# A Perceiver block on one core: self-attention keys and values of six batches as 26 block products, with sums on GpSimd and a new order in the last batch

## Chip, cores and metric
The kernel runs on one core of a Trainium2 chip, as one program. The metric is device time in microseconds (us), the median of the runs of a kernel. In the text TensorE is PE, VectorE is DVE, ScalarE is ACT, GpSimd is POOL and SyncE, which only issues transfers here, is SP; these are the names that the profile uses.

## The reference
Eight batches of 128 rows (width 512) pass three stages, all in float32 with a float8-rounded feed-forward:

```
x = x + xattn(layernorm(x), ctx)      # 8 heads of 64 over 2048 context rows of width 384
x = x + attn(layernorm(x))            # one head, 128 x 128 per batch, causal mask
x = x + ffn(layernorm(x))             # 512 -> 2048 -> 512, relu, e4m3 hidden values and w2

attn:  n = layernorm(x)
       logits = (n @ Wq + bq) @ (n @ Wk + bk).T ; mask above the diagonal
       probs = softmax(logits, axis=1) / sqrt(512)
       x = x + n + probs @ (n @ Wv + bv)
```

The change concerns the middle stage, `attn`: its keys and values.

## The kernel before
**Cross-attention** is a loop over batches b = 0 to 7 and head pairs m = 0 to 3. In each turn PE computes the scores of two heads (L552, 8 matmuls of 64x512), DVE copies them to `p` with running maxima (L556), ACT exponentiates each head in one instruction (L576), DVE transposes 32x32 blocks in place (L589, 8 instructions), and 16 transfers, the strips (L595, 128 KB each), put the blocks in their places in `pT`. `attend` (L607) of this pair comes one turn later on PE, after the scores of the next pair. Its first matmul waits for all 16 strips. `pT` has one buffer. Between `scores` and `attend` the keys and values of the next batch are computed by a block scheme of 20 products (L453, L476), from sums that POOL forms (`sum_half`, L206).

**Self-attention before** folds the query and key weights in one matrix (`both`), so "keys" is `both` times the normalised rows. Class `SelfAttention` works on two groups of four batches. Group 0 (batches 0 to 3): keys as 16 matmuls of 128x512 (L791) in turn m = 1 of the last batch, logits (L806) and three values (L835, 4 matmuls of 128x512 per batch) in turn m = 2. Group 1 (batches 4 to 7): values of 4 and 5 in and after turn m = 3, keys of 4 and 5 and of 6 and 7 as 16 matmuls of 128x256 each; batches 6 and 7 come last, since their rows are ready last. `read` (L858) multiplies probabilities by values. The normalised rows of batches 0 to 5 wait in DRAM (`xtd`, `xr`).

**The feed-forward** uses a block scheme of 26 products for 3/4 of the hidden blocks (`hidden_blocks`, L1162, tables `ROW_SUMS`, `WEIGHT_SUMS`, `PRODUCTS`): a 2x4 by 4x4 block product in 26 instead of 32 block products. It needs 19 sums of rows and 29 of weights (L1133), and its products run through six PSUM banks: a bank takes several products, and between two of them ACT (a block's first use, L1172) or DVE (later ones, L1175) reads it. The first quarter of the hidden units is plain (`hidden`, L1108).

**What sets the order.** PE's order is the order of the code (a manual schedule), and so is that of DVE and ACT. POOL and SP are ordered by a scheduler. Each engine and each queue takes its instructions in order, so an instruction that waits holds up all behind it. PSUM has seven banks for this work (`ps_one`) and one for the output of `attend`.

Around the change the code of the last batch reads, in `if last` branches: turn 0 `v_proj(7,1)` and `project(6)` (L717, output projection of batch 6), turn 1 `sa0.keys`, turn 2 `sa0.weights_and_values`, turn 3 the last loads; then the tail: values, `attend(7,3)`, `project(7)`, normalisation of batch 7 (`stats`, `scale`, `norm`), its keys and logits, the normalised rows of the feed-forward (`turned_rows`, L134), `hidden`, `hidden_blocks`. On DVE the weight and row sums of the feed-forward are placed among the self-attention steps by hand (`some(w_sums, n)`).

Of the kernel before, what the change touches and what calls it, by code (L numbers as in the profile page):

```python
# [65 lines left out]
def tile_perceiver_block(  # L66
# [39 lines left out]
    GT = GB * S  # L106
    RSK = float(D) ** -0.5
# [32 lines left out]
    ktp = ctx.enter_context(tc.tile_pool(name="ktp", bufs=1, side="right"))  # L140
    xa = ctx.enter_context(ExitStack())
# [5 lines left out]
    pp, ptp, tmp, xp = right("pp", 1), right("ptp", 1), right("tmp", TMPB), right("xp", 2)  # L147
# [389 lines left out]
    def scores(b, m):  # L537
# [8 lines left out]
        home, tag = (ktp, "kt0") if (b, m) == (B - 1, 2) else (pp, "p")  # L546
# [175 lines left out]
    rows = {}  # L722
    attention = ctx.enter_context(ExitStack())

    def bring_last_rows():
        rows[0] = keep.tile([P, B, D], F32, tag="keep", name="rows")
        nc.gpsimd.dma_start(rows[0][:, B - 2 :], xd[:, B - 2 :])
        for r in range(B):
            xs[r] = rows[0][:, r, :]

    def bring_rows():
        nc.scalar.dma_start(rows[0][:, : B - 2], xr[:, : B - 2])


    def load_row(pool, src, name):
        t = pool.tile([P, D], F32, tag=name, name=name)
        nc.gpsimd.dma_start(t, src if len(src.shape) > 1 else src.partition_broadcast(P))
        return t

    def load_columns(pool, src, name):  # L740
        t = pool.tile(list(src.shape), F32, tag=name, name=name)
        nc.gpsimd.dma_start(t, src)
        return t

    class SelfAttention:


        def __init__(self, g, lasting, pool, w):
            self.g, self.lasting, self.pool = g, lasting, pool
            self.both, self.swv, self.bv, self.u, self.mask = w  # L750
            self.rows = [g * GB + i for i in range(GB)]
            self.xt = lasting.tile([P, NK, GT], F32, tag=f"xt{g}", name=f"xt_{g}")
            there = slice(g * GT, min((g + 1) * GT, (B - 2) * S))
            nc.gpsimd.dma_start(self.xt[:, :, : there.stop - there.start], xtd[:, :, there])
            self.xn, self.es, self.vals = {}, {}, {}

# [12 lines left out]
        def norm(self, b):  # L769
            mv, sd = self.xn[b]  # L770
            rs = small.tile([P, 1], F32, tag="rs", name=f"rs_s_{b}", bufs=4)
            nc.vector.reciprocal(rs, sd)
            self.xn[b] = self.lasting.tile([P, D], F32, tag="xn", name=f"xn_s_{b}", bufs=GB + 1)
            nc.vector.tensor_scalar(self.xn[b], xs[b], mv[:, 0:1], rs, ALU.subtract, ALU.mult)
            nc.gpsimd.tensor_tensor(xs[b], xs[b], self.xn[b], ALU.add)
            unread = self.pool.tile([P, D], BF16, tag="unread", name=f"unread_{b}")
            row_constant(b, self.xn[b], self.u, unread)

        def turn(self, b):
            turned_into(self.xt, b, self.xn[b], "s")  # L780

        def keys(self, rows):

            at = slice(rows[0] % GB * S, (rows[-1] % GB + 1) * S)
            n = at.stop - at.start
            if at.start == 0:
                self.kt = self.pool.tile([P, NK, GT], F32, tag="sk", name=f"sk_{self.g}")
            for m in range(NK):
                ps = bank(f"psk_{rows[0]}_{m}")
                for k in range(NK):  # L790
                    nc.tensor.matmul(  # L791
                        ps[:, :n], self.both[:, k, ts(m, P)], self.xt[:, k, at],
                        start=(k == 0), stop=(k == NK - 1),
                    )
                nc.scalar.activation(
                    self.kt[:, m, at], ps[:, :n], AF.Identity, bias=side[:, m : m + 1]
                )
                if m == 1:
                    yield

        def logits(self, b):

            i = b % GB
            ps = bank(f"pl_{b}")
            for k in range(NK):
                nc.tensor.matmul(  # L806
                    ps[:, :S], self.kt[:, k, ts(i, S)], self.xt[:, k, ts(i, S)],
                    start=(k == 0), stop=(k == NK - 1),
                )
            lg = self.pool.tile([P, S], F32, tag="lg", name=f"lg_{b}", bufs=4)  # L810
            nc.vector.scalar_tensor_tensor(
                lg, ps[:, :S], c_rows[:, b : b + 1], self.mask, ALU.add, ALU.add
            )
            nm = small.tile([P, 1], F32, tag="snm", name=f"snm_{b}", bufs=4)
            nc.vector.reduce_max(nm, lg, axis=AX.X, negate=True)
            self.es[b] = lg, nm

        def exps(self, b):
            lg, nm = self.es[b]
            e = self.pool.tile([P, S], F32, tag="e", name=f"e_{b}", bufs=4)  # L820
            den = small.tile([P, 1], F32, tag="sden", name=f"sden_{b}", bufs=4)
            nc.scalar.activation(e, lg, AF.Exp, bias=nm, accum_out=den)
            self.es[b] = e, den

        def probabilities(self, b):
            e, den = self.es[b]
            r = small.tile([P, 1], F32, tag="sr", name=f"sr_{b}", bufs=4)
            nc.vector.reciprocal(r, den)
            nc.vector.tensor_scalar(e, e, r, RSK, ALU.mult, ALU.mult)
            self.es[b] = e  # L830

        def values(self, b):
            ps = bank(f"psv_{b}")
            for k in range(NK):
                nc.tensor.matmul(  # L835
                    ps, self.xt[:, k, ts(b % GB, S)], self.swv[:, k, :],
                    start=(k == 0), stop=(k == NK - 1),
                )

            v = self.pool.tile([P, D], F32, tag="sv", name=f"sv_{b}", bufs=GB + 2)  # L840
# [3 lines left out]
        def weights_and_values(self, rows):  # L844
            for r in self.rows:
                self.logits(r)
                self.exps(r)
            for r in rows:
                self.values(r)
            yield  # L850

        def reads(self):
            for r in self.rows:
                self.read(r)

        def read(self, b):
            ps = bank(f"pr_{b}")
            nc.tensor.matmul(ps, self.es[b], self.vals[b], start=True, stop=True)  # L858
            nc.vector.tensor_tensor(xs[b], ps, xs[b], ALU.add)
# [14 lines left out]

    def enter_self_attention():
        src.close()
        sap = ctx.enter_context(tc.tile_pool(name="sap", bufs=1, reuse_waits="tile"))
        wsa = attention.enter_context(tc.tile_pool(name="wsa", bufs=1, reuse_waits="tile"))
        both = wsa.tile([P, NK, D], F32, tag="both", name="both")
        nc.gpsimd.dma_start(both, both_w)  # L880
        w = [both, wsa.tile([P, NK, D], F32, tag="swv", name="swv")]
        sa0 = SelfAttention(0, sap, wsa, w + [None] * 3)
        nc.gpsimd.dma_start(w[1], sa_wv.rearrange("(k p) n -> p k n", p=P))
        w += [load_row(wsa, sa_bv, "bv"), load_row(wsa, u_line, "u")]

        mask = wsa.tile([P, P], F32, tag="mask", name="mask")
        nc.gpsimd.memset(mask, 0.0)
        nc.gpsimd.affine_select(
            out=mask, in_=mask, compare_op=ALU.is_ge, fill=MASKED, base=0,
            pattern=[[1, P]], channel_multiplier=-1,  # L890
        )
        w.append(mask)
        sa0.bv, sa0.u, sa0.mask = w[2:]
        return sap, wsa, w, sa0
# [58 lines left out]
    def normed_group(g, mv, sd, out):  # L953
        rs = small.tile([P, GB], F32, tag="qrs", name=f"frs_{g}")
        nc.vector.reciprocal(rs, sd)
        for i in range(GB):
            xn = sap.tile([P, D], F32, tag="xn", name=f"xn_f_{g}_{i}", bufs=GB + 1)
# [6 lines left out]
    def turned_rows(g, rows, tag):  # L964

        xt = sap.tile([P, NK, GT], F32, tag=tag, name=f"xf_{g}")
# [4 lines left out]
    sa0 = None  # L971
    for b in range(B):
        last = b + 1 == B
        for m in range(NK):
# [12 lines left out]
            if m == 3 and b < B - 2:  # L987
# [4 lines left out]
            elif b > 0:  # L992

                attend(b - 1, NK - 1)
            if m == 0:
# [5 lines left out]
            elif m == 1:  # L1001
                unit = sa0.keys(sa0.rows)
            elif m == 2:
                unit = sa0.weights_and_values(sa0.rows[:3])
            else:

                sa1 = SelfAttention(1, sap, wsa, w)
# [7 lines left out]
            else:  # L1015
                exps(b, m, 0)
                if unit and not (last and m > 0):
                    first_of(unit)
            if m == 3 and last:
                bring_rows()  # L1020
                for r in sa0.rows:
                    sa0.probabilities(r)
                sa1.stats(B - 2)
            exps(b, m, 1)
            if m == 3 and last:
                sa1.scale(B - 2)
            if b == m == 0:
                all_of(both_weights())
            if m == 0 and last:
                bring_last_rows()  # L1030
            if m == 1 and b > 0 and not last:
                row_stats(b - 1)
            if m == 2 and b > 0 and not last:
                norm_rows(b - 1)
            strips = turns(b, m)
# [7 lines left out]
            if m == NK - 1:  # L1043
                if last:
                    inverse_sums(b)
                else:
                    sums_along_rows(b)
            if unit:
                all_of(unit)
# [282 lines left out]
```

## Time and profile before

| | us |
|---|---|
| median of 3 runs | 1078.95 |
| lowest and highest run | 1078.9, 1079.66 |
| the profiled execution: device time | 1078.75 |
| its span, first to last instruction | 1077.0 |
| PE busy | 1069.6 |
| DVE busy | 782.9 |
| ACT busy | 373.4 |
| POOL busy | 262.1 |

All starts below are microseconds from the start of this span. In the tables of instructions each line gives an engine, a line of the kernel, an operation, out<-in with shapes and a count; then the busy time, the mean duration of one in ns, and the idle time just before, with what ended it. A float32 matmul appears as two matmul records, so x32 is 16 matmuls. The granted clock is 1.000 throughout.

### The profile page before, as it was taken

How to read it: one execution, taken by the hardware profiler on the slowest of the kernel's cores; microseconds unless marked ns; L12 is line 12 of the kernel's file. 1: busy time of each engine (PE TensorE's matmuls, PEld its weight loads, DVE VectorE, ACT ScalarE, POOL GpSimd, SP SyncE). 2: the span in 40 equal slices, each digit the busy share in tenths (PEclk: the TensorE clock that was granted, in tenths of full speed). 3: DMA queues.
4: the chain of work that ended last, by engine and by line, in shares of the span. 5: the costliest groups of instructions: out<-in, count | busy, mean ns of one | idle time of the engine just before them, and what ended most of it. 6: DMA issues, size and time to landing. Idle time of an engine off the chain costs nothing.

```text
span 1077.0 us, 15773 instructions
## 1 busy us (share of the span) xinstructions
PE 1069.6 (99%) x5586; PEld 701.0 (65%) x5586; DVE 782.9 (73%) x1724; ACT 373.4 (35%) x608; POOL 262.1 (24%) x397
## 2 busy tenths in 40 slices
PE   9999999999999999999999999999999999999998
PEld 5475784577467647754775578557746655758775
DVE  4876477778777778787778768777877758686654
ACT  3322233324332433432343234332433232256442
POOL 0254140361055005500550153026200221104000
PEclk9999999999999999999999999999999999999999
DMA  8466434553565456545643653455344745530001
GB/s 321 147 187 145 129 79 98 147 148 79 127 165 137 96 131 165 137 95 134 161 124 79 183 146 83 118 147 147 79 98 118 230 136 154 205 108 10 11 30 40
DMA packets 74031, 136.64 MB, mean 127 GB/s; under 512 B 29392, under 2 KB 37856, under 8 KB 72928
## 3 DMA queue, kind: packets, MB, share of 16 engines
q1 hardware_dynamic: 60736, 108.83, 39.5%
q10 hardware_dynamic: 9008, 15.73, 4.5%
q0 software_dynamic: 4208, 11.06, 3.5%
q8 instruction: 45, 0.74, 0.3%
q14 instruction: 34, 0.28, 0.1%
HBM read 55.85 MB, written 10.52 MB: 62 GB/s over the span
## 4 chain that ended last, share of the span: by engine, by line
PE 97%; DVE 1%; SPq 1%; ACT 1%; issue 0%; DMA 0%; POOL 0%; ACTq 0%; POOLq 0%
PE pv_z L476 22%; PE pk_z L453 20%; PE po L607 11%; PE sc L552 10%; PE ph L1162 7%; PE pv_b L476 4%; PE pk_b L453 3%; PE psk L791 3%; PE psv L835 3%; PE pq L520 3%; PE py L717 3%; PE pf L1190 2%; PE k L436 2%; PE ph L1108 1%; PE pw L336 1%; SPq L325 1%
## 5 line engine op out<-in xcount | busy, mean ns | idle before, releaser
L589 DVE STREAM_TRANSPOSE p<-p 128x512 f32<-128x512 f32 x256 | 158.9, 679 | 62.7 <-ACT p L576 62.7
L576 ACT ACTIVATE p<-p,nm 128x2048 f32<-128x2048 f32 x64 | 128.2, 2003 | 210.7 <-DVE nm L564 103.8
L556 DVE TENSOR_SCALAR_CACHE_REDUCE p<-sc 128x512 f32<-128x512 f32 x256 | 159.0, 686 | 20.7 <-PE sc L552 20.3
L476 PE MATMUL pv_z<-wv_sums,x_both 128*128 128x256 f32 x640 | 157.9, 381 | 0.0
L453 PE MATMUL pk_z<-x_both,wk_sums 128*128 128x512 f32 (+1 forms) x320 | 149.2, 572 | 0.9 <-ACT kt L369 0.6
L476 PEld LDWEIGHTS pv_z<-wv_sums,x_both 128*128 128x128 f32 x640 | 120.4, 190 | 18.6 <-issue 2.9
L607 PEld LDWEIGHTS po<-pT,v 128*64 128x64 f32 x2048 | 111.1, 137 | 23.8 <-issue 23.1
L607 PE MATMUL po<-pT,v 128*64 128x128 f32 x2048 | 118.9, 274 | 0.0
L552 PE MATMUL sc<-kt,q 64*128 64x512 f32 x512 | 118.5, 602 | 0.0
L476 PE MATMUL pv_z<-wv_sums,m_both 128*128 128x256 f32 x448 | 107.3, 379 | 0.0
L453 PEld LDWEIGHTS pk_z<-x_both,wk_sums 128*128 128x128 f32 x320 | 59.2, 190 | 67.1 <-issue 55.0
L453 PE MATMUL pk_z<-m_both,wk_sums 128*128 128x512 f32 (+1 forms) x224 | 101.3, 568 | 0.0
L629 POOL DMA_DIRECT2D line_s<-inverse x28 | 14.5, 526 | 352.4 <-DVE inverse L626 352.4
L206 POOL TENSOR_TENSOR m_both<-x_both 128x256 f32<-128x256 f32 x70 | 51.3, 733 | 172.7 <-DMA x_both<-in_ctx_t_dram 141.9
L476 PEld LDWEIGHTS pv_z<-wv_sums,m_both 128*128 128x128 f32 x448 | 84.2, 190 | 12.6 <-POOL x_both L206 0.8
L552 PEld LDWEIGHTS sc<-kt,q 64*128 64x128 f32 x512 | 46.8, 186 | 65.7 <-issue 54.3
L369 ACT COPY v<-pv_z 128x512 f32<-128x512 f32 x112 | 62.9, 586 | 56.1 <-PE pv_z L476 56.0
L369 ACT COPY kt<-pk_z 128x512 f32<-128x512 f32 (+1 forms) x112 | 59.8, 563 | 58.1 <-PE pk_z L453 57.7
L571 ACT COPY seen<-mx 128x1 f32<-128x1 f32 x21 | 4.0, 191 | 208.7 <-DVE p L556 208.7
L206 POOL TENSOR_TENSOR x_both<-x_both 128x256 f32<-128x256 f32 x98 | 70.7, 739 | 3.7 <-DMA x_both<-in_ctx_t_dram 3.6
L453 PEld LDWEIGHTS pk_z<-m_both,wk_sums 128*128 128x128 f32 x224 | 40.8, 190 | 46.8 <-issue 35.1
L372 DVE TENSOR_TENSOR v<-pv_z,v 128x512 f32<-128x512 f32 x96 | 63.1, 685 | 5.5 <-PE pv_z L476 5.5
(218 smaller groups left out, 1369.8 us busy)
## 6 DMA issues: line engine op xcount, KB each, us to landing
pT<-p SPq DMA_DIRECT2D x488, 128.0 KB, 2.4
x_both<-in_ctx_t_dram SPq DMA_DIRECT2D x45, 512.0 KB, 5.2
w<-in_w_t_dram ACTq DMA_DIRECT2D x2, 2048.0 KB, 11.3
w2f<-in_w_t_dram SPq DMA_DIRECT2D x16, 256.0 KB, 3.4
pT<-p POOLq DMA_DIRECT2D x24, 128.0 KB, 4.0
x_in<-in_x_dram SPq DMA_DIRECT2D x8, 256.0 KB, 6.5
qd<-xq SPq DMA_DIRECT2D x8, 256.0 KB, 3.0
q<-qd SPq DMA_DIRECT2D x8, 256.0 KB, 4.1
```

Source lines behind the costliest of these rows:

```text
L206: eng.tensor_tensor(x_block(b, h, to), x_block(b, h, one), x_block(b, h, two), ALU.add if op == "+" else ALU.subtract,)
L369: nc.scalar.copy(outs[ij], views(ps))
L372: nc.vector.tensor_tensor(outs[to], views(ps), outs[other], op)
L453: nc.tensor.matmul(ps[:, : n * BK], wk_sums[:, WSLOT[WAT[r]], f2, :], x_block(b, hs, XAT[r]), start=start, stop=True, skip_group_check=True,)
L476: nc.tensor.matmul(ps[:, ts(t, 256)], x[:, ts(t, P)], wv_sums[:, WSLOT[WAT[r]], :], start=start and t == 0, stop=True, skip_group_check=True,)
L520: nc.tensor.matmul(ps, wq[:, k, ts(m, P)], xt[:, k, :], start=(k == 0), stop=(k == NK - 1),)
L552: nc.tensor.matmul(pair[i], q[r, :], kts[b, m // 2][r, m % 2, ts(n, 512)], start=True, stop=True)
L556: nc.vector.tensor_scalar(p[:, :, i].rearrange("p g (t i) -> p t g i", i=SQ)[:, ts(n, Q)], pair[i].rearrange("p (t g i) -> p t g i", g=Q, ...
L576: nc.scalar.activation(p[:, :, i], p[:, :, i], AF.Exp, bias=nms[b, m][:, i : i + 1], scale=SCALE, accum_out=sums[b][:, h : h + 1],)
L589: nc.vector.transpose(p[:, g, i], p[:, g, i])
L607: nc.tensor.matmul(pos[b][h * DH : (h + 1) * DH, ts(m, P)].rearrange("p (a i) -> p a i", a=Q), v[:, jt % 8, ts(2 * m + h, DH)], turned_[b, ...
L1162: nc.tensor.matmul(banks[at][:, ts(t, HR)], w_at(of_w, d), x_at(g, of_x), start=start and t == 0, stop=True, skip_group_check=True,)
```

## The change
1. Keys and values of batches 0 to 5 (768 rows, two blocks of 384) are computed by the scheme of 26 products that the feed-forward has. Keys: 26 matmuls of 128x384 in turn m = 1 of the last batch. Values: 26 products of three matmuls of 128x128 each, in turn m = 3. The generator `product_blocks` is now shared with the feed-forward.
2. The sums that these products need (19 of rows, 29 of weights for the keys, 29 for the values) are made on POOL; one row sum that subtracts twice stays on DVE. The weights are summed in place, so plain `both` and `swv` are loaded a second time for batches 6 and 7, whose keys are now 16 matmuls of 128x128 each.
3. The self-attention tiles have no pools of their own: they are slices of `x_both`, `m_both`, `wk_sums` and `wv_sums`, which are free then. POOL and SP are ordered by hand from turn 0 of the last batch.
4. The last batch is rearranged: `project(6)` goes from the end of turn 0 to turn 1, ahead of the keys; batch 6 is normalised in turn 2 with its keys there; logits stand ahead of the strips' transposes in turns 2 and 3; reads 0 to 3 go behind `attend(7,3)`; `p` of turn 3 instead of turn 2 lies in a key tile.
5. In the tail fewer of the feed-forward's weight sums come ahead of `read`; the row sums start behind the last `read`.

The core of the diff, lines of the kernel after:

```diff
-        home, tag = (ktp, "kt0") if (b, m) == (B - 1, 2) else (pp, "p")
+        home, tag = (ktp, "kt0") if (b, m) == (B - 1, 3) else (pp, "p")
...
+    def product_blocks(name, mm, take, more, whole=None):
+        banks, taken, left = {}, set(), {}
+        for *_, reads in PRODUCTS:
+            for i, j, _ in reads:
+                left[i, j] = left.get((i, j), 0) + 1
+        for at, start, of_x, of_w, reads in PRODUCTS:
+            if start:
+                banks[at] = bank(f"{name}_{at}")
+            mm(banks[at], of_x, of_w, start)
+            for i, j, sign in reads:
+                (more if (i, j) in taken else take)(i, j, banks[at], sign)
+                taken.add((i, j))
+                left[i, j] -= 1
+                if whole and left[i, j] == 0:
+                    whole(i, j)
+            yield
...
+            for k in (2, 0, 1, 3):
+                nc.sync.dma_start(self.xt_six[:, k], xtd[:, k, :SIX])
+                nc.sync.dma_start(self.both[:, k], both_w[:, k])
...
+        def sum_w(self, w, some):
+            for to, one, op, two in some:
+                add_up(nc.gpsimd, self.w_at(w, to), self.w_at(w, one), op, self.w_at(w, two))
...
+        def keys_of_six(self):
+            def mm(ps, of_x, of_w, start):
+                nc.tensor.matmul(ps[:, :HALF], self.w_at(self.both, of_w), self.x_at(of_x),
+                    start=start, stop=True, skip_group_check=True)
+            def take(i, j, ps, sign):
+                nc.scalar.activation(self.kt_six[:, j, ts(i, HALF)], ps[:, :HALF], AF.Identity,
+                    bias=side[:, j : j + 1], scale=float(sign))
+            def more(i, j, ps, sign):
+                to = self.kt_six[:, j, ts(i, HALF)]
+                nc.vector.tensor_tensor(to, to, ps[:, :HALF], ALU.add if sign > 0 else ALU.subtract)
+            return product_blocks("psk", mm, take, more)
+        def values_of_six(self):
...
+                for t in range(3):
+                    nc.tensor.matmul(ps[:, ts(t, P)], x[:, ts(t, P)], self.w_at(self.swv, of_w),
+                        start=start and t == 0, stop=True, skip_group_check=True)
...
+            def whole(i, j):
+                for t in range(3):
+                    to = self.v_six[:, 3 * i + t, ts(j, P)]
+                    nc.gpsimd.tensor_tensor(to, to, self.bv[:, ts(j, P)], ALU.add)
...
+        def logits_and_keys(self):
+            self.turn(6)
+            self.logits(0)
+            yield
+            for b in range(1, 4):
+                self.logits(b)
+            self.keys(6, self.kts[6])
+            for b in range(4):
+                self.exps(b)
+            for b in range(4):
+                self.probabilities(b)
+        def logits_and_values(self):
+            for b in (4, 5):
+                self.logits(b)
+            yield
+            yield from self.values_of_six()
...
+            if m == 1 and last:
+                project(b - 1, ot)
...
-                unit = sa0.keys(sa0.rows)
+                unit = sa.keys_of_six()
             elif m == 2:
-                unit = sa0.weights_and_values(sa0.rows[:3])
+                unit = sa.logits_and_keys()
             else:
+                unit = sa.logits_and_values()
...
+            if m == 1 and b > 0:
+                (sa.stats if last else row_stats)(b - 1)
...
+            if m > 1 and last:
+                first_of(unit)
             strips = turns(b, m)
...
+            if m == 1 and last:
+                sa.scale(b - 1)
+                nc.scalar.activation(warm, eps, AF.Exp)
+                sa.load_plain(sa.both, both_w)
+                sa.sum_w(sa.swv, WEIGHT_SUMS)
...
-    some(w_sums, 16)
-    all_of(sa1.keys(sa1.rows[2:]))
...
+    sa.probabilities(B - 1)
+    xfs = [turned_rows(0, xf0, k_flat[:, : NK * GT])]
+    sa.read(B - 2)
     quantized = quantize_w2()
     hidden(0, xfs[0], range(1))
     some(quantized, 2)
-    for r in sa1.rows[2:]:
-        sa1.read(r)
...
+    sa.read(B - 1)
+    forms = wff.tile([P, 18, HR], F32, tag="x_forms_0", name="x_forms_0")
+    x_sums = form_x(0, xfs[0], [forms[:, i] for i in range(18)], nc.vector)
+    some(w_sums, 4)
     for _ in w_sums:
         some(x_sums, 1)
     all_of(x_sums)
```

## The prediction
> **What bounds the kernel now.** I read the table of busy time first, then the chain of waits, then the timeline and the stretches around the change.
>
> ```profile
> PE 1069.6 (99%) x5586; PEld 701.0 (65%) x5586; DVE 782.9 (73%) x1724; ACT 373.4 (35%) x608; POOL 262.1 (24%) x397
> ...
> PE 97%; DVE 1%; SPq 1%; ACT 1%; issue 0%; DMA 0%; POOL 0%; ACTq 0%; POOLq 0%
> ```
>
> PE is the bound, also in the chain. The chain's pieces (start, us, what) from 799 to 963.4 are PE alone, without a gap; some of them:
>
> ```profile
> 855.15 13.93 PE psk L791 x32
> 869.08 3.63 PE sc L552 x16
> 872.71 3.65 PE po L607 x64
> 876.36 3.77 PE pl L806 x32
> 880.13 10.30 PE psv L835 x24
> 890.43 3.63 PE sc L552 x16
> 894.06 3.64 PE po L607 x64
> 897.71 10.50 PE psv L835 x24
> ...
> 965.68 0.28 ACT sum L1172
> 965.96 0.04 issue
> 966.00 14.08 PE ph L1162 x64
> ```
>
> So a matmul saved here is worth its full time, and any new wait of PE here costs its full time: no slack is there to absorb it. The question is which is more.
>
> **What PE saves.** Keys and values take 13.93 + 10.30 + 10.50 in these pieces and 3.45 + 3.46 + 3.43 + 3.48 + 6.91 in five smaller ones behind them: 55.46 us. A matmul with 512 columns takes 13.93/16 = 0.870, with 256 columns 6.91/16 = 0.432, with 128 columns (`pl`) 0.89/4 = 0.224: proportional. After: 26 of 384 columns by 0.645 (three quarters of 0.86) = 16.8; 78 of 128 by 0.224 = 17.5; keys of batches 6 and 7, 32 by 0.224 = 7.2; their values 3.43 + 3.48 = 6.9. Sum 48.4, **7.1 less** (6.1 if a matmul of 128 columns costs 0.01 more than `pl` shows). PE's other matmuls stay the same in number; those moved cost what they did.
>
> **The new sums on POOL: nothing.** Not shown at these sizes. POOL's 128x256 sums take 0.735 and its 128x512 additions 1.274, which gives 0.46 for 128 columns and 1.0 for 384 by a line through them (0.23, as its `MEMSET` of 128x128, to 0.74 are the bounds of the first, 0.74 to 1.27 of the second). 16 row sums, 29 weight sums and two operations of the mask: about 31 us (20 to 44). Their loads (2.6 MB) go out on SP at about 820, when batch 7's key sums are used up, and by the 250 to 300 GB/s of the stretches below need 9 to 10 us. From 825 to 856, then. The keys begin at 855.1, since `project(6)` in front of them only changes place with them, take the sums in the order in which POOL makes them, and use the last at 871: 15 us of cover. The 29 sums of the value weights (13 us from 864) are used from 900 on, and the 24 bias additions (11 us) end by 922, before the first read at 923. Plain `both` comes back in 7 us after 871 and is used at 883.
>
> **The new waits on PE.** S is the start of scores(7,2), 873.2 with the sums so far and wait 1 below; R is the end of `rb`, about 923.2. DVE takes its instructions in the written order, and behind a turn's transposes come all the additions that free the banks.
>
> 1. Keys of six, **1.4** (0.9 to 1.9). On DVE the addition of `py` (waits for 855.1), statistics and the eight transposes of turn (7,1) (4.86, 856.7 to 861.6) stand ahead of the first addition, which ends at 862.1. The tenth product writes the same bank; PE would be there at 860.9.
> 2. `turn(6)`, **0.9** (0.5 to 1.2). It waits for `norm(6)` and its row constant, on DVE behind eight evictions of scores: ready at S + 8.0 and a hop; PE has done scores and attend at S + 7.3.
> 3. attend(7,2), **3.4** (2.0 to 4.5), the largest. The transfers that feed an attend now:
>
> ```profile
> 877.71 4.86 DVE L589 STREAM_TRANSPOSE p<-p 128x512 f32<-128x512 f32 x8 [2.16 <-ACT p L576]
> 882.86 2.89 POOL L595 DMA_DIRECT2D pT<-p  x6 [0.56 <-DVE lg L811]
> 893.99 3.71 PE L607 MATMUL po<-pT,v 128*64 128x128 f32 x64
> ```
>
> Columns: start, us, engine. And the stretches at that time, DMA share and GB/s last:
>
> ```profile
> 886.00:888.00 2.00, 2.00 (x6) 0.93 (x5) 0.69 (x1) 0.00 (x0) 0.00 (x0) 1.00 1.06 301
> 888.00:890.00 2.00, 2.00 (x6) 0.76 (x4) 0.00 (x0) 0.00 (x0) 0.00 (x0) 1.00 1.02 236
> 890.00:892.00 2.00, 2.00 (x9) 0.88 (x10) 1.17 (x2) 0.00 (x0) 0.00 (x0) 1.00 0.15 33
> ```
>
> The strips have landed near 890.1, 12.4 after the first transpose, 4 before they are needed. In that turn 25 us lie between the starts of scores and of this attend, filled by attend, logits and three values. After, scores, attend, `turn` 0.44, four logits 3.77, 3.58 of keys(6), the 0.9 above and scores(7,3) put PE there at S + 19.5. The first transpose stood 8.7 after the scores' start; now `norm(6)` and logits(0), which waits for PE's first `pl`, come first, so that it starts at S + 10.3. Add 12.4: S + 22.7, and a hop. PE waits 3.3 to 3.5. Should the strips land quicker in the quieter stretch it is 2; with POOL's strips held up by its weight sums, 4.5.
> 4. Values of six, **0.2** (0 to 1): logits 4 and 5 stand ahead of the transposes of turn (7,3), which end 5.5 us into the values; as in wait 1, but without `py`.
> 5. `ph_0`, **1.8** (0.5 to 2.5). PE's work between R and it: reads 0 to 3 3.43, `py` 3.43, reads 4 and 5 1.72, values 6.9, `turn` 0.44, logits 1.8, keys 3.58, `pt_f` 1.75, read(6) 0.86 = 23.9. ACT does exp(7) ahead of its copies of `pt_f`, and exp(7) waits for DVE's logits(7) behind ten weight sums of 0.55: R + 22.9. exp 0.4 and four copies (2.05 now) with their hops: R + 25.7.
> 6. First block of `hidden_blocks`, **3.4** (2.0 to 4.5). Now:
>
> ```profile
> 953.39 1.28 DVE L859 TENSOR_TENSOR rows<-pr,rows 128x512 f32<-128x512 f32 x2
> ...
> 960.87 0.42 DVE L1133 TENSOR_TENSOR x_forms<-x_forms,xf 128x256 f32<-128x256 f32 x1
> 961.21 1.28 DVE L942 BATCH_NORM_STATS2 fst<-rows 128x6 f32<-128x512 f32 x2
> ...
> 966.00 1.99 PE L1162 MATMUL ph<-x_forms,w_forms 128*128 128x256 f32 x8 [0.88 <-ACT sum L1172]
> ```
>
> Behind the last read DVE now has six weight sums, eleven row sums and statistics, ready 1 us before PE needs them. After, all 19 row sums and 19 weight sums stand behind read(7), a pair in 0.805 by the starts of these lines (0.47 + 0.34): 15.6, and 1.9 for the addition and statistics. read(7) ends one quarter of `hidden` after `ph_0`'s start; three quarters, 10.3, remain. The additions that the tenth product waits for (its bank again) come at 8.0 after the block's start; PE is there at 5.0 (968.70 now, from 963.43). That is 2.9, and 0.5 for the products behind.
>
> Sum: 1.4 + 0.9 + 3.4 + 0.2 + 1.8 + 3.4 = 11.1 of waits, less 7.1: **+4.0**. The profiled run took 1078.75 (span 1077.0 and 1.75 around it), so 1082.75; the median of before is 0.2 above that run, so about **1082.8**.
>
> [...]
>
> **The rivals.**
> - *Strips in time* (16%). Wait 3 falls, for the strips could land in 9 us rather than 12.4: 2.1 MB at the 301 GB/s of the stretch above are 7 us. Against it: the issuing itself, 16 strips over two queues, took until 886 now. 1082.8 - 3.4 = **1079.4**, no change.
> - *DVE's queue is not late at PE* (9%, faster). Waits 1, 2, 3, 4 and 6 (9.3) are all differences between an order on DVE and PE's arrival; if DVE runs 3 us further ahead than I place it, they go, and -7.1 + 1.8 = -5.3 remains: **1073.6**. It decides from waits of DVE under 5.3 in sum. For it: DVE is 73% busy. Against it: the transposes can't start before the exponentials, which hang on PE's scores, not on DVE's load.
> - *POOL late* (6%, slower). The loads come late or the sums take the upper bound, 44: the last ends at 870 rather than 856, each product waits in turn, and everything from the keys on shifts by up to 8: **1090** and more. It decides when the sums end past 868. Against it: the 15 us of cover.
> - That the change does not do what it says is excluded: 26 and 78 matmuls stand in PE's order.
>
> **How the numbers follow.** The forecast has the rest, 69%. Its lows are waits of 5.9 less 7.2, its highs waits of 15.6 less 6.1: from 1078.75 and with the 0.2, 1077.6 to 1088.5. That range also holds the even case, so that 15% is left out. 1076.8 to 1081.1 is within 0.2%, about what a measurement can tell from no change. Faster: 9%, the second rival. Same: 16%, the first. Slower: 69 + 6 = 75%.
>
> **What would show it.** In the profile after: `psk` and `psv` together at 48.4 on PE; PE idle 1.4 before the tenth key product, ended by DVE; 0.9 at `pt_s`, ended by DVE; 3.4 at attend(7,2), ended by a strip's DMA; 1.8 at `ph_0`, ended by ACT's copy of `xf`; 3.4 in the first `hidden_blocks`, ended by DVE; the last POOL row or weight sum of the keys near 856. Strips(7,2) landed by S + 19.5, or the last row sum within 2 us of the block's start, would make it wrong on the fast side; PE waiting for POOL at `psk` on the slow side.

## The result, and the profile after

The changed kernel takes **1089.22 us** (median of 4 runs, 1088.38 to 1091.89) against 1078.93 before: ratio 1.010, 95% interval 1.008 to 1.012, slower. The forecast was 1082.8 with a range of 1077.6 to 1088.5: the sign was right, the size was not. The profiled execution took 1088.51, span 1086.7, so 9.7 more than the 1077.0 before.

The page of the kernel after, busy time and chain:

```profile
PE 1067.4 (98%) x5714; PEld 710.8 (65%) x5714; DVE 798.2 (73%) x1755; ACT 380.0 (35%) x623; POOL 309.9 (29%) x488
...
PE 92%; DVE 5%; SPq 1%; DMA 1%; ACT 1%; issue 0%; POOL 0%; DVEq 0%; POOLq 0%
```

PE is busy only 2.2 us less, not 7.1, and the chain now runs 5% through DVE and 1% through a transfer. Who made PE wait from 840 to 1000, total, times, longest (before, this list held one line, 0.9 in the first product block):

```profile
PE po L611 <- DMA pT<-p: 5.8, 1, 5.8
PE ph L1264 <- DVE x_both L1277: 2.6, 1, 2.6
PE ph L1219 <- ACT wk_sums L137: 1.4, 1, 1.4
PE psk L863 <- DVE x_both L876: 1.2, 1, 1.2
PE ph L1264 <- DVE w L738: 0.9, 1, 0.9
PE pt_s L854 <- DVE pt_s L715: 0.8, 1, 0.8
PE psv L954 <- DVE mv_s L833: 0.2, 1, 0.2
```

All five places of the forecast with a wait of any size are there, with the releasers that it named. The first is the large one. Its transposes and its attend in the timeline (start, us, idle before in brackets):

```profile
883.93 4.86 DVE L593 STREAM_TRANSPOSE p<-p 128x512 f32<-128x512 f32 x8
...
899.68 6.12 PE L611 MATMUL po<-pT,v 128*64 128x128 f32 x64 [5.82 <-DMA pT<-p]
905.73 2.05 PE L931 MATMUL pl<-x_both 128*128 128x128 f32 x16
```

The same 64 records of attend take 3.71 in every other turn, 6.12 here. Stretches of 2 us (PE busy first; the last three columns are granted clock, share of the transfer engines, GB/s):

```profile
892.00:894.00 2.00, 1.86 (x6) 0.48 (x3) 2.00 (x8) 0.00 (x0) 0.46 (x1) 1.00 1.00 261
894.00:896.00 2.00, 0.00 (x0) 0.00 (x0) 2.00 (x7) 0.00 (x0) 0.00 (x0) 1.00 1.07 276
896.00:898.00 2.00, 0.00 (x0) 0.00 (x0) 1.29 (x6) 0.60 (x1) 0.00 (x0) 0.96 0.97 238
898.00:900.00 2.00, 0.32 (x4) 0.35 (x6) 0.00 (x0) 2.00 (x3) 0.00 (x0) 0.50 0.00 0
900.00:902.00 2.00, 2.00 (x22) 2.00 (x20) 0.00 (x0) 1.48 (x2) 0.00 (x0) 0.50 0.79 197
902.00:904.00 2.00, 2.00 (x23) 2.00 (x21) 0.00 (x0) 0.00 (x0) 0.00 (x0) 0.50 0.97 412
904.00:906.00 2.00, 2.00 (x29) 1.83 (x26) 0.00 (x0) 0.00 (x0) 0.00 (x0) 0.84 0.46 186
```

Two things are to be seen. The stretches show no traffic behind 898, but PE starts only at 899.68. The chain has what lies between (start, us, what):

```profile
892.93 5.98 DMA pT<-p
898.91 0.78 issue
899.68 6.12 PE po L611 x64
```

The last strip goes out at 892.93, its landing is noted at 898.91, and PE starts 0.77 behind it: the end of the traffic in the stretches is not yet the landing. And while PE stood idle here its granted clock fell to 0.50, and stayed there for 5 us after it had started again; PE is "busy" from 900 on, but at the pace of these 6.12. In the profile of before the clock is 1.00 throughout.

In numbers, profile against profile:

| step | forecast | measured |
|---|---|---|
| matmuls of keys and values (17.0 + 17.7 + 7.3 + 6.9 = 48.9) | -7.1 | -6.6 |
| 1, tenth key product | 1.4 | 1.2 |
| 2, `turn(6)` | 0.9 | 0.8 |
| 3, attend(7,2): wait | 3.4 | 5.8 |
| 3: half clock (attend 6.12 for 3.65) | none | 2.5 |
| 3: logits behind it, at full clock (1.98 for 1.79) | 0 | 0.2 |
| 3: scores(7,3) ahead of it (4.46 for 3.70) | 0 | 0.8 |
| 4, values of six | 0.2 | 0 |
| 5, `ph_0` | 1.8 | 1.4 |
| 6, first product block (2.55 and slower hand-overs) | 3.4 | 3.0 |
| reload of `swv` (0.15 of waiting, `values(6)` 3.67 for 3.43) | 0 | 0.4 |
| sum | +4.0 | +9.5 (9.7 in the spans) |

Step 3 is 5.9 above its forecast, the whole sum 5.5; the rest nearly cancels. For the 0.2 at `values(6)` the list of waits names DVE's `mv_s`, which ended at 938.31; the reload of `swv` landed at the same time.

### The profile page after: what moved, and what is told of

It is laid out like the page before. It is cut to its first block, busy times and chain, and to the rows that moved or that the text cites. A ratio compares the mean times of both kernels' runs of the same rounds, so it can differ in the third digit from the quotient of the medians.

```text
span 1086.7 us, 16247 instructions
## 1 busy us (share of the span) xinstructions
PE 1067.4 (98%) x5714; PEld 710.8 (65%) x5714; DVE 798.2 (73%) x1755; ACT 380.0 (35%) x623; POOL 309.9 (29%) x488
## 4 chain that ended last, share of the span: by engine, by line
PE 92%; DVE 5%; SPq 1%; DMA 1%; ACT 1%; issue 0%; POOL 0%; DVEq 0%; POOLq 0%
PE pv_z L480 21%; PE pk_z L457 20%; PE po L611 11%; PE sc L556 10%; PE ph L1264 7%; PE pv_b L480 4%; PE pk_b L457 3%; PE py L721 3%; PE pq L524 3%; PE pf L1293 2%; PE k L440 2%; PE psv L891 2%; PE pw L340 1%; PE psk L863 1%; DVE p L593 1%; SPq L329 1%
## 5 line engine op out<-in xcount | busy, mean ns | idle before, releaser
L611 PEld LDWEIGHTS po<-pT,v 128*64 128x64 f32 x2048 | 113.6, 139 | 29.5 <-issue 28.6
L611 PE MATMUL po<-pT,v 128*64 128x128 f32 x2048 | 121.3, 277 | 5.8 <-DMA pT<-p 5.8
```

What stands on the lines that cost most here:

```text
L611: nc.tensor.matmul(pos[b][h * DH : (h + 1) * DH, ts(m, P)].rearrange("p (a i) -> p a i", a=Q), v[:, jt % 8, ts(2 * m + h, DH)], turned_[b, ...
```

## The experiments

**Theory A**: the new waits of PE are matters of order on DVE, ACT and the transfers, an idle PE loses half its clock on top, and the saving of 6.6 is real. Rivals: **B**, the slow attend comes from what runs beside it, not from PE's idle time; **C**, the transfers and not their start set when the strips land; **D**, the scheme brings its cost with it, wherever its sums and loads are put. The runs of the kernel before beside them gave medians of 1078.7 to 1079.2.

**Filling PE's idle time**, with 26 matmuls, and with 12 in a second run.

```diff
+            if m == 3 and last:
+                idle = bank("idle")
+                for _ in range(26):
+                    nc.tensor.matmul(idle[:, :P], ident, ident, start=True, stop=True)
             if m > 0:
                 attend(b, m - 1)
```

> 26 matmuls of 128x128 (5.8 us) whose result nobody reads stand on PE between scores(7,3) and attend(7,2), where PE is idle for 5.8 us in the changed kernel. Theory A (PE's idle time is what halves the granted clock, which then makes attend and what follows slower): the granted clock stays 1.00 from 880 to 930, attend(7,2) takes 3.65 instead of 6.12, the two logits 1.79 instead of 1.98, and the time falls by 2.6 to about 1086.6, although PE does more. Rival B (the slow attend comes from something else at that time: the transfer of 1.5 MB of rows that runs beside it, or PE reading what has just landed): attend stays at 6.1 and the time at 1089.2 or above.

> The same with 12 matmuls (2.7 us), so that 3.1 us of idle time remain ahead of attend(7,2). In the changed kernel the clock fell about 3.9 us after PE's last matmul. Theory A with a point at which it decides: 3.1 us are not enough, the clock stays 1.00, attend takes 3.65 and the time is about 1086.6, as with 26. If instead the loss of clock grows with the idle time in proportion, about half of the 2.6 stays: 1087.9. Rival B: 1089.2.

1090.78 and 1092.47 (ratios 1.010 and 1.012). With 26, the timeline of PE:

```profile
893.36 6.07 PE L1098 MATMUL idle<-ident 128*128 128x128 f32 x52
899.36 3.71 PE L611 MATMUL po<-pT,v 128*64 128x128 f32 x64
903.00 2.05 PE L931 MATMUL pl<-x_both 128*128 128x128 f32 x16
...
937.84 5.37 PE L954 MATMUL psv<-m_both,wv_sums 128*128 128x512 f32 x8 [2.28 <-DMA m_both<-in_sa_wv_dram]
```

The same attend, after the same transfers and beside the same 1.5 MB, takes 3.71 once PE has had something to do: B is refuted, and the half clock comes from the idle time. Yet the expected gain of 2.6 is missing in the time. The two logits kept their 1.98 at full clock, so they have no part in what the clock cost. PE reached `values(6)` 2.7 earlier and there met a wait that the changed kernel only touches (0.2): plain `swv` is reloaded after the last value product, and in the changed kernel its 1 MB goes out at 925.55, 2.7 behind 4 MB of feed-forward weights, and takes 12.8 to land. 2.3 of waiting, and half clock again: 5.37 for 3.67. In the first product block PE lost pace too behind a wait of 2.56 (six matmul records 2.54 for 1.46), where the clock had stayed up behind 2.55 in the changed kernel (1.00 from 976 to 984). With 12 the idle time was 2.64 and the clock fell all the same (0.50 from 899 to 902, attend 5.03), so the point of decision that I had written down, 3.9 us, is wrong.

**Logits behind the transposes** (turn 2).

```diff
-            if m > 1 and last:
+            if m == 3 and last:
                 first_of(unit)
             strips = turns(b, m)
```

> Undoes one part of the change: in turn (7,2) DVE's logits(0) stands behind the eight transposes, not ahead of them. Theory A (DVE's order starts the strips too late): the transposes start at about 882.6 instead of 883.93, the strips land 1.3 earlier, the wait at attend(7,2) is 4.5 instead of 5.8; the clock still falls, so that 1.3 to 2 of the time goes: 1087.2 to 1087.9. Rival C (the transfers, not their start, set the landing: they share the transfer engines with the 256 KB row of batch 7): the wait shortens by under 0.5 and the time stays at 1089.

1088.57 (1.009, 1.007 to 1.011). The wait fell to 4.9 and the profiled span by 1.3, but the medians' intervals overlap: the time is inconclusive. The transposes started 2.2 earlier (881.74), 0.9 of it because this execution's scores did (872.75 for 873.65), and from the first transpose to attend it took 16.1 instead of 15.8. So an earlier start brings an earlier landing, as A has it, but 0.9 of the wait rather than 1.3 went; C has a part in it.

**Batch 7's row later.** `load_x(7)` goes from the beginning of turn 3 behind the values.

> Of the changed kernel only the load of batch 7's row (256 KB) is moved from the time of the strips of turn (7,2) to the end of turn 3. Theory A (this row was moved on the same transfer engines between the strips): the strips land about 1 us earlier, the wait at attend(7,2) is 4.8 instead of 5.8; time 1088. If the strips' own 2.1 MB and their issue set the landing, the wait stays at 5.8.

1089.37 (1.010), but the wait at attend(7,2) is 4.2 instead of 5.8:

```profile
PE po L611 <- DMA pT<-p: 4.2, 1, 4.2
PE ph L1265 <- DVE x_both L1278: 2.9, 1, 2.9
```

The row is the part of C: its 256 KB between the strips cost 1.7. From the first transpose (883.83) to attend (897.90) it is now 14.1 instead of 15.8. The time gained nothing, because the wait of 2.9 in the product block now brought half clock in turn (0.58 from 976 to 980), and `values(6)` waited 1.3. The waits stand in a row behind each other: taking one away early lets PE run sooner into the next.

**Weight sums in the gaps**: the tail alone.

```diff
     sa.probabilities(B - 1)
+    some(w_sums, 3)
     xfs = [turned_rows(0, xf0, k_flat[:, : NK * GT])]
...
     some(quantized, 2)
+    some(w_sums, 6)
     sa.read(B - 1)
```

> Three more weight sums ahead of read(6) and six between read(6) and read(7) on DVE, where it waits for PE in the changed kernel (4.6 us busy of the 10 from 950 to 960); nine fewer behind read(7). Theory A (step 6 of the forecast: the sums behind the last read are late): the last sum ends 4.2 earlier, the 2.55 of waiting in the first product block go, and 0.5 with them: 1086.2. Rival: the waits in that block come from the hand-over of PSUM banks and not from the sums: they stay and the time is 1089.2.

1085.88 (1.006, 1.0045 to 1.0075): as expected. The 2.6 are gone from the list of waits and only the 0.9 that the kernel before has too is left in that block; `values(6)` waited 1.5 for the reload in this execution. Step 6 is confirmed, and DVE's idle time around the last two reads was room enough.

**The whole tail in order**; the last two lines stand beside the load of the rows in turn 3.

```diff
-    sa.exps(B - 1)
-    some(w_sums, 2)
-    sa.probabilities(B - 1)
     xfs = [turned_rows(0, xf0, k_flat[:, : NK * GT])]
+    sa.exps(B - 1)
+    some(w_sums, 5)
     sa.read(B - 2)
+    sa.probabilities(B - 1)
...
     some(quantized, 2)
+    some(w_sums, 6)
...
+                w1 = [None, ktp.tile([P, 2, HID], F32, tag="kt1", name="w1_1")]
+                nc.scalar.dma_start(w1[1], w1_t.rearrange("(i k p) n -> i p k n", i=2, p=P)[1])
```

> Only the tail of the changed kernel is reordered: the weight sums of the gaps as before (ten more ahead of the last read in all), exp(7) behind the four copies of turned rows on ACT, and the second half of the feed-forward's weights (2 MB) loaded 18 us earlier, so that the reload of plain swv has the transfer engines to itself. Theory A (steps 5 and 6, and the reload that I left out): 3.0 of the first product block, 1.4 at ph_0 and the 0.2 to 2.4 at psv go, against the changed kernel: 1084 to 1085. If the reload's wait only moves to the weight sums, which need the loads too, 1086.

1083.29 (1.004, 1.003 to 1.006). All that is left of PE's waits:

```profile
PE po L611 <- DMA pT<-p: 5.7, 1, 5.7
PE psk L863 <- DVE x_both L876: 1.2, 1, 1.2
PE ph L1264 <- DVE x_forms L738: 0.9, 1, 0.9
PE pt_s L854 <- DVE pt_s L715: 0.8, 1, 0.8
```

`ph_0`, the product block and the reload are clean. 5.9 of the 10.3 by which the changed kernel is slower came from the tail.

**The front, by splitting the keys.** The last nine key products go behind scores(7,2), logits 0 to 5 into turn 2, `project(6)` between the key products, `norm(6)` ahead of scores(7,2).

```diff
+            if m == 2 and last:
+                all_of(keys_left)
             if m > 0:
                 attend(b, m - 1)
...
+                for i in range(9):
+                    next(unit)
+                project(b - 1, ot)
+                sa.stats(b - 1)
+                for i in range(9, 16):
+                    next(unit)
+                sa.scale(b - 1)
...
+                sa.norm(b - 1, xp.tile([P, D], F32, tag="x", name=f"xn_s_{b - 1}"))
```

> Only the front is reordered: project(6) behind the ninth key product, normalisation of batch 6 inside the keys, the last nine key products behind scores(7,2), logits 0 to 5 in turn 2, transposes ahead of logits, sums of the value weights behind the strips of turn (7,2) on POOL. So 8 us more of PE's work lie between the strips' start and attend(7,2). Theory A (the new waits are matters of order, and the scheme's saving of 6.6 is real): waits 1, 2 and 3 and the half clock go (10.4), scores(7,2) with three free banks costs 1 to 2, the first value products 1: about 1081. Rival D (the scheme brings its cost with it, through POOL's sums and transfers, wherever they stand): new waits of the same size, 1088 to 1090.

> Both rearrangements together. Theory A: 1075 to 1078, faster than before the change. Rival D: 1083 or above.

1087.65 (1.008) for the front alone, next to D's number, and 1081.89 (1.0035, 1.002 to 1.005) with the tail, between the two. A's number is missed in both. The profile says by what: attend(7,2) no longer waits, but scores(7,2) waited 1.9 for DVE, which normalised batch 6 first, with half clock behind it (0.50 from 874 to 876); the fifth key product 1.2 to 1.5 for a sum of POOL or for its bank; and with the tail, attend(7,3) 2.3 for strips that shared with rows and weights, with half clock again (0.50 from 925 to 928, attend 5.38). New waits in place of the old, then; whether order can take them away too is left open by this pair. Mended (norm behind the first late key additions, `project(6)` behind the fourth product, weights before and rows behind the strips, batch 7's row later):

> The version with both rearrangements (1081.9), whose own new waits are mended: project(6) behind the fourth key product (covers 1.5), normalisation of batch 6 behind the first of the late key additions (1.9 at scores(7,2) and about 1.7 of half clock), the 2 MB of weights at the start of turn 3 and the 1.5 MB of rows behind the strips (2.3 at attend(7,3) and 1.7 of half clock), batch 7's row later. Left are about 1.2 for scores with three free banks and 1.1 at the fifth value product. Theory A: 1075.5 to 1077.5, faster than before the change. Rival D (the scheme brings its cost with it wherever it stands): 1080 or above.

1078.11 (0.9997, 0.9989 to 1.0006): no difference from before. The wait at attend(7,3) is gone, but scores(7,2) still waited 2.8 (0.50 from 872 to 876), and not for the normalisation. The first eviction on DVE:

```profile
870.28 0.69 DVE L560 TENSOR_SCALAR_CACHE_REDUCE p<-sc 128x512 f32<-128x512 f32 x1 [3.35 <-DMA pT<-p]
```

It waited 3.35 for the strips of turn (7,1) to leave `p`, which turns 1 and 2 share since the change put `p` of turn 3, not of turn 2, into the key tile. Splitting the keys brings scores(7,2) too early for that.

**The front without splitting.** From the version with the tail in order (`norm` stands behind the 21st key product; batch 7's row goes behind the exponentials of turn (7,3)):

```diff
+                for i in range(4):
+                    next(unit)
+                project(b - 1, ot)
...
+                sa.norm(b - 1, xp.tile([P, D], F32, tag="x", name=f"xn_s_{b - 1}"))
...
             self.turn(6)
-            self.logits(0)
-            yield
-            for b in range(1, 4):
+            for b in range(6):
                 self.logits(b)
+                self.exps(b)
+            yield
             self.keys(6, self.kts[6])
```

> The simpler way, without splitting the keys: the tail of the run with the reordered tail (1083.3), and in front logits 4 and 5 in turn 2 (1.8 more of PE's work ahead of attend(7,2)), all logits behind the transposes (0.9), batch 7's row later (1.6), project(6) behind the fourth key product and normalisation of batch 6 inside the keys (1.2 and 0.8). Theory A: the wait at attend(7,2) falls from 5.7 to 1 or 2, too short for the clock to fall, and the time to 1075 to 1077. Rival D: 1080 or above, with new waits in place of the old.

1077.52 (0.9992, 0.9983 to 1.000): just above A's range, and hardly to be told from before. Attend(7,2) waited 2.1, long enough for half clock here (0.50 from 896 to 898, attend 5.38), attend(7,3) 1.0. Then

```diff
+            if m == 2 and last:
+                early_values = sa.values_of_six()
+                for _ in range(3):
+                    next(early_values)
...
+            if m == 3 and last:
+                nc.sync.dma_start(rows[:, :6], xr[:, :6])
```

> The simpler way again (1077.5), with what its own trace still shows at the two attends taken away: the first three value products (2.0 us, none of which DVE has to read) ahead of scores(7,3), so that PE reaches attend(7,2) when its strips have landed (2.1 of waiting and 1.7 of half clock now), and the 1.5 MB of rows behind the strips of turn (7,3), so that attend(7,3) does not wait (1.0 now). Four banks are left to scores(7,3), which may cost 0.4. Theory A: 4.4 less than the profiled 1076.7 of that run, 1072 to 1074, faster than before the change by the scheme's 6.6 less one. Rival D (waits move, they do not go): 1076 or above.

1077.11 (0.998, 0.997 to 0.9992): less gain than A expected, and within D's range. Attend(7,2) is clean, and the wait moved to attend(7,3) (2.2) and to the tenth value product (1.5), which PE now reaches before DVE has done with the transposes. Last, the weights ahead of the exponentials of turn (7,3):

```diff
+            if m == 3 and last:
+                w1 = [None, ktp.tile([P, 2, HID], F32, tag="kt1", name="w1_1")]
+                nc.scalar.dma_start(w1[1], w1_t.rearrange("(i k p) n -> i p k n", i=2, p=P)[1])
             unit = None
```

> The version with three early value products (1077.1), with the 2 MB of the feed-forward's weights issued on ACT ahead of the exponentials of turn (7,3), 2 us earlier, so that they are through when the strips of that turn start. Theory A (the 2.2 of waiting at attend(7,3) is a matter of what shares the transfer engines with the strips): the wait falls to 1 or less and the time to 1075 to 1076.5. If the 1.5 MB of rows behind the strips are what holds them, the wait and the time stay.

**1075.31** (0.9966, 0.9954 to 0.9978), faster than both kernels. Busy time on its page, its chain, and PE's waits from 800 to 1000:

```profile
PE 1064.9 (99%) x5714; PEld 709.4 (66%) x5714; DVE 798.1 (74%) x1755; ACT 379.0 (35%) x623; POOL 309.6 (29%) x488
...
PE 96%; DVE 2%; SPq 1%; ACT 1%; issue 0%; DMA 0%; POOL 0%; POOLq 0%
```

```profile
PE psv L893 <- DVE x_both L903: 1.5, 1, 1.5
PE ph L1268 <- ACT x_both L1277: 0.9, 1, 0.9
```

The same matmuls, the same sums on POOL, the same bytes as the changed kernel, 13.9 us less. PE's clock is 1.00 in every stretch from 880 to 932, and 0.999 in the mean of this execution. D is refuted: with the scheme unchanged, another order of instructions and transfers took away all of the new waits but 1.5.

## Why the prediction was wrong, step by step

- *What PE saves*: 6.6 for 7.1. The proportional price held (17.0 for 16.8, 17.7 for 17.5, 7.3 for 7.2). The 6.1 of the forecast, 110 matmuls at 0.01 more, should have read 6.0.
- *Sums on POOL, nothing*: right. A 128x128 sum took 0.46, a 128x384 sum 1.00, as drawn from the line; the last of the keys' sums ended at 858.6 for 856, since POOL made 18 row sums and not the 16 that the forecast counted, 2.0 more. PE waited for POOL nowhere in the changed kernel from 800 on. One row of the trace of before came back. There, at 929.6, a POOL addition took 1.77 where its twin took 1.28, beside a DVE line (`c_rows`) of 1.10 where the others take 0.16; after the change `c_rows` took 1.05 on DVE beside POOL's 1.78. DVE then stood idle 0.71 before its next instruction, so it cost nothing on the path, and the eight transposes kept their 4.86.
- *Waits 1, 2, 4, 5, 6*: 1.2, 0.8, 0, 1.4 and 3.0 for 1.4, 0.9, 0.2, 1.8 and 3.4, each that came with the releaser named. In 6 two slips of the sum add up: 19 pairs of 0.805 are 15.3 and not 15.6, and from 963.43 to 968.70 it is 5.3 and not 5.0. By its own rows the wait was about 2.4 rather than 2.9; 2.55 came. Reading the order of DVE beside PE's arrival was the right method; 5 and 6 went when the order was mended.
- *Wait 3 is the step that failed*: "Add 12.4: S + 22.7, and a hop. PE waits 3.3 to 3.5." The transposes did start at S + 10.3 (883.93 for S of 873.65). But from the first transpose to attend it took 15.8 and not 12.4. The forecast took the landing for the place where the traffic thins out in its stretches (890.1), though the last of its three lines still shows a share of 0.15 and 33 GB/s. The trace of before notes the landings themselves: the last strip went out at 887.19 and landed at 891.84, 14.1 after the first transpose. In turns (7,1) and (7,3) it was 14.2 and 13.8. This reading alone is 1.7 of the 3.4 that are missing. Another 0.9 came with batch 7's row between the strips, which the forecast left out; before the change, that row was loaded with batch 6's in turn 0, at 825.8 (in the run with the row later, attend itself starts 14.1 behind the first transpose). The last 0.8 lies between the landing and PE's start, where the forecast has "a hop". PE also came 0.7 later than S + 19.5, as scores(7,3) waited for evictions: hence 5.8. My upper end for this wait was 4.5.
- *No term for the clock*: each wait was priced at its length. This one cost 2.5 more, in attend. The forecast's sentence "any new wait of PE here costs its full time" put too little on it. The trace of before could not show such a cost: its list has no wait of PE over 0.9 from 800 to 1000. The runs show one: behind waits of 2.1 and 2.3 attend took 5.38 for 3.71, 1.7 more. They also show that the length of a wait alone did not give it: the clock fell behind waits of 1.9 and stayed up behind one of 2.55 (last section).
- *Reload of `swv`*: priced at nothing, 0.2 of waiting in the profiled run, up to 2.4 where PE arrived earlier.
- *The rivals*: the slower side was right, by another mechanism than the POOL that I named. "DVE's queue is not late at PE" did not come by itself, as the forecast had argued; where the order was mended until 1.5 of new waits were left, the kernel gains 3.4. That is 6.6 less those 1.5, less 1.2 at scores(7,3), which took 4.87 there for 3.70; no run assigns the remaining 0.5.

What stays open: where the other runs of the changed kernel lost their time, which scatters over 3.5 us (before: 1.5). The clock has a part in it: the four runs, from 1088.38 to 1091.89, have a mean granted clock of 0.997, 0.996, 0.995 and 0.995, and 0.001 of the span is 1.1 us. The runs without a profile don't show in which place it fell.

## What to carry to other kernels

Where one engine is the bound without a gap, a saving there is worth only what the new order leaves of it: list each place where the bound engine will meet another engine's queue or a transfer, and price the wait, with the clock that an idle PE lost here (2.5 us more in one attend). Time a transfer from its trigger to the landing that the trace notes for its last part, and on to the start of what waits for it; the place where the traffic thins out was 1.7 us too early here. And mend waits from the last to the first: an early one that was taken away here delivered PE sooner to the next.

## What the runs showed of the hardware

In the profiled executions, from 840 to 1000, PE's granted clock fell to 0.50 behind every wait of 2.8 us and more (2.8, 2.9, 2.9, 4.2, 4.9, 5.6, 5.7, 5.8), behind nine of the twelve between 1.9 and 2.6, and behind none of 1.6 or less. It fell 1.7 (tail in order) to 4.0 us (row later) after PE's last matmul and came back 2.7 (12 fillers) to 6.6 us (mended split) after PE had started again. Half clock lasted 6.8 us behind the 5.8 of the changed kernel (897.8 to 904.7) and 3.4 behind the 2.6 with 12 fillers (898.7 to 902.1).

The twelve, and the longest wait below them. The times of half clock are worked out from the mean clock of the stretches; "-" is a place outside of them, where the work behind the wait alone tells it.

| wait | half clock, from and to | work behind it |
|---|---|---|
| 2.64, attend(7,2), 12 fillers | 898.7 to 902.1 | 5.03 for 3.71 |
| 2.56, first product block, 26 fillers | - | six records 2.54 for 1.46 |
| 2.56, the same place, 12 fillers | - | six records 2.45 for 1.46 |
| 2.56, the same place, logits behind the transposes | - | six records 1.46 |
| 2.55, the same place, changed kernel | none | six records 1.46 |
| 2.38, `values(6)`, 12 fillers | - | 5.37 for 3.67 |
| 2.30, attend(7,3), split with the tail | 924.6 to 928.0 | 5.38 for 3.71 |
| 2.28, `values(6)`, 26 fillers | - | 5.37 for 3.67 |
| 2.23, attend(7,3), three early value products | none | 3.71 |
| 2.08, attend(7,2), logits early | 895.4 to 898.8 | 5.38 for 3.71 |
| 1.89, scores(7,2), front split | 873.2 to 876.6 | ten records 4.60, where sixteen take 3.70 |
| 1.89, the same place, split with the tail | 873.4 to 876.8 | ten records 4.60 |
| 1.63, `values(6)`, front split | none | 3.67 |

So the same wait cost now its own length and now more: 2.3 at attend(7,3) brought 1.7 more in the split with the tail, and 2.2 there brought nothing with three early value products. The runs of one kernel differ in the clock too, though only one of them has a profile: of the eleven of the mended split version four have a mean clock of 1.000 (1076.54 to 1077.87), seven have 0.996 to 0.998 (1077.83 to 1081.26). What decides whether the clock falls behind a wait of 1.9 to 2.6, and when it comes back, these runs do not show.
